# Transposes ahead of the maxima, output rows' transposes in the maxima's banks, and half a step between offset and scaling

## The chip, the cores and the metric

The kernel runs on one core of one Trainium2 chip. The metric is the device time of one execution in microseconds (us). The kernel before took 1583.12 us, the median of three runs (1580.37 to 1586.11).

The engines are named as in the profile: PE multiplies matrices (PEld loads its weights), DVE is the vector engine, ACT the scalar engine, POOL the general one, and SP issues DMAs. PE writes its results into PSUM, which has eight banks of 128 x 512 float32. DVE and ACT read them from there.

## What is computed

The input is `x` of 8 batches x 1024 rows x 256 columns. Every batch is computed by itself:

```python
xn = _layernorm(x, axis=-1)
s = _L0_attn_ref(xn, L0_attn_W_attn, L0_attn_b_attn, L0_attn_W_proj, L0_attn_b_proj)
g = _silu(_L0_ffn_ref(xn, L0_ffn_w_gate, L0_ffn_w_up, L0_ffn_w_down))
x = x + s * g
```

`_L0_attn_ref` is causal attention with 16 heads of 16 columns, with a rotation of queries and keys that (as the reference reads its axes) depends on the head, and a softmax. `_L0_ffn_ref` is a gated feed-forward with 768 hidden columns and integer weights: `silu(gate) * up`, then the down projection.

## The kernel before

**Groups and steps.** The 16 heads of a batch are worked on in 4 groups of 4, so there are 32 groups in all, strung in one chain. `attention` (L660) works on one group in 12 steps `n`: 4 blocks of keys for the first half of the queries, 8 for the second. A step has two pairs of heads, and a pair has two quarter steps, so a group has 48 quarter steps. The queries' exact row maxima are needed before the exponentials, so while group `i` computes its weights (`pw`, L562, then the exponential `e` on ACT, L569), the same quarter steps compute the maxima of group `i + 1` (`pm`, L504). `quarter_steps` (L641) spreads the 38 units of maxima over the 48 quarter steps, at most one in each. A unit is one bank of scores: PE writes it, DVE reduces it (L513 for a block of keys that lies wholly before the queries, L515 with the mask for the others).

**What a quarter step issues, in this order:** the weights of a bank; pieces of other work (`slot(weights)`); the unit of maxima, if there is one; in a few quarter steps a small transposition (below); again pieces of other work (`slot(maxima)`). The order is written out by hand, and each engine executes its own instructions in that order. At the end of a pair one entry of `vector` is run (a piece of the next batch's layer norm). After every second step the products of exponentials and values of two steps follow (`av`, L598).

**The small transposes.** `shift_queries` (L537) turns the row maxima of half of a group's queries into rows: one transpose `pq` (L540), a copy to `rows` on ACT (L542), and two small DMAs from SP into the queries' array `q_st` (L544). It runs twice per group, in the second quarter step of steps 2 and 7. `finish` (L611) takes the sums `avs` of a half of a group: four transposes `py` (L616), then on DVE a reciprocal `rec` (L618) and a product `y` (L619). It is called through `endings`, in the last quarter step of steps 1 and 5.

**Banks.** Eight banks are divided in four pools: two for `pw`, three for the maxima (`max_tile`, L72), one for `av`, and two for everything else (`fill_tile`, L75). `pq` and `py` take banks of the maxima. A tile can be written only when the earlier tile in its bank has been read by its last reader. `fill_tile` first calls `flush()`, which issues the DVE work that was put off in the list `later` (for example the gate `th`, L352, that reads a bank `ph`). `maxima` calls `flush()` too, behind its own reductions.

**The other work** is one long list `chain` of pieces, taken in order when they are due by the planner's costs (`slot`, L823): projections of the next batch (`pqk` L234, `pv` L267), the feed-forward (`ph` L325, whose readers are ACT L337 and L341 and then DVE L352; `pd` L379, read by ACT L390 and DVE L391), and the output of the batch before in four pairs of row tiles. `transpose_y` (L408) opens a pair: a DMA of `res`, four transposes `pyt` (L417) into one bank of the pool of two, and a copy `yT` on ACT (L423). `project_out` (L425) multiplies it (`po`, L432). Pairs 1, 2 and 3 are each followed in the chain by pieces of the feed-forward: pair 1 by `pd`, pairs 2 and 3 by `ph`.

**The norm of the next batch.** `norm_steps` (L94) returns a list of entries, one for each half step: eight of statistics (DVE), `first`, three `step` (POOL from the second batch on), `offset` (POOL, L127 and L128), and eight of `scale`, which run on ACT from the second batch on (L137) and read what `offset` wrote.

Of the kernel before, what the change touches and what calls it, by code (L numbers as in the profile page):

```python
# [35 lines left out]
def gated_block_kernel(ctx: ExitStack, tc: tile.TileContext, x, wqk, wv, bv, wp, bp, wg, wu, wd, rope, out):  # L36
# [3 lines left out]
    CC = C // P  # L40
# [23 lines left out]
    def flush(keep=0):  # L64
        while len(later) > keep:
            later.pop(0)()

    def cast(keep=0):
        while len(casts) > keep:
            casts.pop(0)()  # L70

    def max_tile(name):  # L72
        return ps_pm.tile([P, HALF], F32, tag="pm", name=name)

    def fill_tile(name):  # L75
        flush()
        return ps_fill.tile([P, HALF], F32, tag="fill", name=name)
# [16 lines left out]
    def norm_steps(b):  # L94


        stats = {}

        def one(t):
            if t == 0:  # L100
                stats["mv"] = small.tile([P, NT, 2], F32, tag="mv", name=f"mv_{b}")
            st = small.tile([P, 6], F32, tag="st", name=f"st_{b}_{t}")
            nc.vector.bn_stats(out=st, in_=xs[:, t, :])
            nc.vector.bn_aggr(out=stats["mv"][:, t, :], in_=st)

        def first():

            var, rstd, t = (small.tile([P, NT], F32, tag=tag, name=f"{tag}_{b}") for tag in ("var", "rstd", "newton"))
            stats["root"] = var, rstd, t
            nc.vector.tensor_scalar(var, stats["mv"][:, :, 1], LN_EPS, None, ALU.add)  # L110
            nc.vector.tensor_scalar(rstd.bitcast(I32), var.bitcast(I32), -0.5, float(0x5F3759DF), ALU.mult, ALU.add)

        def step():
            var, rstd, t = stats["root"]
            if b == 0:
                nc.vector.tensor_tensor(t, rstd, rstd, ALU.mult)
                nc.vector.scalar_tensor_tensor(t, t, -0.5, var, ALU.mult, ALU.mult)
                nc.vector.scalar_tensor_tensor(rstd, t, 1.5, rstd, ALU.add, ALU.mult)
                return
            nc.gpsimd.tensor_tensor(t, rstd, rstd, ALU.mult)  # L120
            nc.gpsimd.tensor_tensor(t, t, var, ALU.mult)
            nc.gpsimd.tensor_scalar(t, t, -0.5, 1.5, ALU.mult, ALU.add)
            nc.gpsimd.tensor_tensor(rstd, rstd, t, ALU.mult)

        def offset():
            _, rstd, t = stats["root"]
            nc.gpsimd.tensor_tensor(t, stats["mv"][:, :, 0], rstd, ALU.mult)  # L127
            nc.gpsimd.tensor_scalar(t, t, -1.0, None, ALU.mult)  # L128

        def scale(i):  # L130
            _, rstd, t = stats["root"]
            if b == 0:
                nc.vector.tensor_scalar(
                    xs[:, i, :], xs[:, i, :], stats["mv"][:, i, 0:1], rstd[:, i : i + 1], ALU.subtract, ALU.mult
                )
            else:
                nc.scalar.activation(  # L137
                    xs[:, i, :], xs[:, i, :], AF.Identity, bias=t[:, i : i + 1], scale=rstd[:, i : i + 1]
                )
            scaled[b] = i + 1  # L140

        tiles = range(NT)
        return [
            *[lambda t=t: one(t) for t in tiles],
            *[first, step, step, step],
            *([offset] if b else []),
            *[lambda t=t: scale(t) for t in tiles],
        ]

# [59 lines left out]
    class Batch:  # L209
# [198 lines left out]
        def transpose_y(self, pair):  # L408
            b = self.b
            assert self.complete[pair // 2] == GROUPS  # L410
            self.res[pair] = p2.tile([P, 2, C], F32, tag="res", name=f"res_{b}_{pair}")
            nc.sync.dma_start(out=self.res[pair], in_=x[b, ts(pair, 2 * P), :].rearrange("(t p) d -> p t d", p=P))
            py = fill_tile("pyt").rearrange("p (c n) -> p c n", c=CC)
            for c in range(CC):
                for i in range(2):
                    t = 2 * pair + i
                    nc.tensor.transpose(py[:, c, ts(i, P)], self.y[t // QT][:, t % QT, ts(c, P)], ident)  # L417
            if (b, pair) == (NB - 1, NT // 2 - 1):

                self.yT[pair] = pe.tile([P, 2, HALF], F32, tag="e", name=f"yT_{b}_{pair}")[:, :, : 2 * P]  # L420
            else:
                self.yT[pair] = p1.tile([P, CC, 2 * P], F32, tag="yT", name=f"yT_{b}_{pair}")
            nc.scalar.copy(self.yT[pair], py)  # L423
# [207 lines left out]
    def add_values(count):  # L631
        for _ in range(count):
            of, half, kb, es = waiting.pop(0)
            ending = of.values(half, kb, es)
            if ending:
                endings.append(ending)
# [23 lines left out]
    def attention(groups, at, plan, slot, vector):  # L660

        group = groups[at]
        after = groups[at + 1] if at + 1 < len(groups) else None
        loaded = groups[at + 2] if at + 2 < len(groups) else None
        plan = iter(plan)
        for n, (half, kb) in enumerate(group.weight_steps()):
            es = []
            for pair in range(2):
                e, banks = group.weights(half, kb, pair)
                es.append(e)  # L670
                for second, bank in enumerate(banks):
                    weights, maxima, units = next(plan)
                    if bank:
                        bank()
                    cast()
                    slot(weights)
                    for unit in units:
                        after.maxima(*unit)
                    if not units:
                        flush()  # L680
                    if pair == 0 and second and n == 2:
                        group.shift_queries(1)
                    if pair == 0 and second and n == QT + 3 and after:
                        after.shift_queries(0)
                    if pair == 1 and second and endings:
                        endings.pop(0)()
                    slot(maxima)
                if vector:
                    vector.pop(0)()
            waiting.append((group, half, kb, es))  # L690
            if len(waiting) == 3:
                add_values(2)
            for entry in delayed:
                entry[0] -= 1
            while delayed and delayed[0][0] <= 0:
                delayed.pop(0)[1]()
            if n == QT - 1 and after:
                after.shift_parts(0)
            if n == STEPS - 1 and after:
                after.shift_parts(1)  # L700
            if loaded:
                if n == QT - 1:
                    loaded.load(0, 0)
                elif n == 2 * QT - 1:
                    loaded.load(1, 0)
                elif n == STEPS - 1:
                    loaded.load(0, 1)
                    loaded.load(1, 1)
# [14 lines left out]
    def forward(exact, general=None):  # L723
# [88 lines left out]
        for b in range(NB):  # L812

            here = range(b * GROUPS, (b + 1) * GROUPS)
            for i in here:
                open_group(groups, batches, i + 2)
            plans = [quarter_steps(groups[i], groups[i + 1] if i + 1 < len(groups) else None) for i in here]
            total = sum(w + m for plan in plans for w, m, _ in plan) + sum(us for us, _ in chain[done[0] : marks[b + 1]])
            slots = 2 * sum(len(plan) for plan in plans)
            due, spent, at = [0.0], [0.0], [0]  # L820
            vectors = []

            def slot(before):  # L823
                due[0] += total / slots
                spent[0] += before
                at[0] += 1
                while (
                    done[0] < (marks[b + 1] if b + 1 < NB or batches[b].complete[0] == GROUPS else marks[b + 1] - 6)
                    and spent[0] + chain[done[0]][0] / 2 <= due[0]
                ):  # L830
                    spent[0] += chain[done[0]][0]
                    run(1)
                if at[0] == 8 and b < NB - 1:
                    if b:
                        load_x(b + 1)
                    vectors.extend([lambda: None] * 5 + norm_steps(b + 1))

            for i, plan in zip(here, plans):
                attention(groups, i, plan, slot, vectors)
                groups[i] = None  # L840
            run(marks[b + 1] - done[0])
# [160 lines left out]
```

## Time and profile before

| | |
|---|---|
| median of the runs | 1583.12 us |
| the profiled execution, its time / its span | 1587.18 / 1585.4 us |
| PE busy | 1507.6 us, 95% of the span |
| DVE busy | 1085.5 us, 68% |
| ACT busy | 959.4 us, 61% |
| POOL busy | 740.7 us, 47% |
| granted PE clock, mean | 0.990 |
| DMA, share of 16 engines | 43.4% for the main queue |
| `pq` L540: instructions, mean | 64, 271 ns |
| `py` L616: instructions, mean | 256, 274 ns |
| `pyt` L417: instructions, mean | 128, 272 ns |
| copies to `rows` L542 / `yT` L423, median | 250 / 587 ns |
| `rec` L618 / `y` L619, median | 250 / 424 ns |
| `scale` on ACT, L137: instructions, median | 56, 602 ns |

Busy is the union of an engine's instructions. A row of a group of instructions gives their number, the busy time, the mean of one in ns, and then the idle time of the engine just before them with what ended it. A line of the timeline gives start, duration, engine, line and operation, the tile written and those read, and in brackets the idle time before it with its releaser. Where one matmul follows another closely, their recorded spans overlap, so the distance between their starts says more than the durations.

### The profile page before, as it was taken

The page shows a single profiled execution, that of the slowest core. Times are in us where ns is not written, and L with a number is a line of the kernel's source. Part 1 is how long each engine was busy: PE and PEld are TensorE (multiplying, and loading weights), DVE is VectorE, ACT ScalarE, POOL GpSimd, SP SyncE. Part 2 cuts the span into 40 slices and gives each one's busy share as a digit, 9 for nine tenths or more (in the row PEclk, how much of TensorE's full clock was granted, in tenths as well). Part 3 has the DMA queues.
Part 4 walks back from the last instruction along what each step waited for, and adds up shares of the span by engine and source line. Part 5 has one row for each costly group of instructions (what it writes and reads, how often), then busy time and mean ns, then how long its engine had stood idle before and what let it go on. Part 6 is the DMA issues. An engine that isn't in the chain of part 4 may idle for free.

```text
span 1585.4 us, 29513 instructions
## 1 busy us (share of the span) xinstructions
PE 1507.6 (95%) x9801; PEld 1054.3 (66%) x9801; DVE 1085.5 (68%) x3284; ACT 959.4 (61%) x2076; POOL 740.7 (47%) x1443
## 2 busy tenths in 40 slices
PE   4889999999999999999999999999999999999997
PEld 2567667676677766776666766767666676666664
DVE  6876776767767677776667666776676767777742
ACT  2256665576656666566655766657665666656664
POOL 4554443554436443464434734355343544434353
PEclk9999999999999999999999999999999999999999
DMA  6812554334464255543346344444455335445301
GB/s 180 185 29 41 108 106 76 76 55 104 98 104 65 51 106 97 98 75 67 94 77 111 58 95 95 75 94 62 94 108 88 68 49 110 93 75 81 48 15 43
DMA packets 92086, 132.86 MB, mean 84 GB/s; under 512 B 13714, under 2 KB 41874, under 8 KB 91923
## 3 DMA queue, kind: packets, MB, share of 16 engines
q1 hardware_dynamic: 90944, 129.82, 43.4%
q8 instruction: 80, 1.31, 0.4%
q10 hardware_dynamic: 978, 1.05, 0.3%
q14 instruction: 84, 0.68, 0.2%
HBM read 87.82 MB, written 41.94 MB: 82 GB/s over the span
## 4 chain that ended last, share of the span: by engine, by line
PE 85%; DVE 4%; ACT 4%; POOL 2%; issue 2%; DMA 2%; SPq 1%; DVEq 0%; ACTq 0%; POOLq 0%
PE pw L562 20%; PE av L598 17%; PE pm L504 16%; PE ph L325 11%; PE pqk L234 6%; PE pd L379 6%; PE po L432 3%; PE pv L267 3%; ACT e L569 2%; PE py L616 2%; DVE trash L515 1%; DMA qk<-high 1%; PE pxt L225 1%; PE pq L540 1%; DVE low L249 1%
## 5 line engine op out<-in xcount | busy, mean ns | idle before, releaser
L569 ACT ACTIVATE e<-pw 128x512 f32<-128x512 f32 (+2 forms) x1280 | 678.7, 558 | 427.8 <-PE pw L562 396.8
L515 DVE CUSTOM_DVE_ANT_0 trash<-pm,mask_q 128x128 bf16<-128x128 f32 (+3 forms) x1024 | 501.3, 490 | 336.0 <-PE pm L504 297.0
L562 PE MATMUL pw<-q_st,k_st 67*128 67x512 f32 (+3 forms) x1536 | 554.3, 394 | 8.0 <-ACT e L569 5.5
L504 PE MATMUL pm<-k_st,q_st 65*128 65x512 f32 (+3 forms) x1536 | 520.9, 377 | 6.9 <-DMA qk<-high 3.7
L562 PEld LDWEIGHTS pw<-q_st,k_st 67*128 67x128 f32 x1536 | 277.7, 189 | 205.6 <-issue 100.3
L576 POOL TENSOR_SCALAR_AFFINE_SELECT e<-e 128x256 f32<-128x256 f32 x512 | 206.6, 408 | 437.0 <-ACT e L569 435.3
L513 DVE TENSOR_REDUCE top_far<-pm 128x1 f32<-128x512 f32 x512 | 338.6, 684 | 70.3 <-PE pm L504 69.1
L504 PEld LDWEIGHTS pm<-k_st,q_st 65*128 65x128 f32 x1536 | 279.6, 191 | 57.7 <-issue 17.2
L598 PE MATMUL av<-e,v_sb 128*32 128x512 f32 (+3 forms) x3072 | 293.1, 499 | 0.3 <-POOL e L576 0.3
L356 POOL TENSOR_TENSOR th<-th,ups 128x256 f32<-128x256 f32 x192 | 140.5, 732 | 231.5 <-DVE th L352 225.4
L598 PEld LDWEIGHTS av<-e,v_sb 128*32 128x32 f32 x3072 | 81.0, 110 | 133.6 <-issue 100.6
L360 POOL TENSOR_TENSOR h_low<-th,h_high 128x256 fp32r<-128x256 f32 x192 | 140.7, 733 | 15.4
L234 PE MATMUL pqk<-xnT,wqk_sb 128*128 128x512 f32 x256 | 133.9, 609 | 0.3 <-DVE bqk_sb L912 0.3
L325 PE MATMUL ph<-xnT_high,wg_sb 128*128 128x256 f32 x384 | 102.1, 288 | 12.0 <-DVE th L352 9.0
L379 PE MATMUL pd<-wd_sb,h_high 128*128 128x256 f32 x384 | 99.0, 286 | 7.9 <-ACT yT L423 4.7
L352 DVE SCALAR_TENSOR_TENSOR th<-th,ph 128x256 f32<-128x256 f32 x192 | 79.7, 415 | 31.2 <-ACT ups L341 30.8
L325 PE MATMUL ph<-xnT_high,wu_sb 128*128 128x256 f32 x384 | 101.1, 285 | 0.0
L379 PE MATMUL pd<-wd_sb,h_low 128*128 128x256 f32 x384 | 98.3, 285 | 1.7 <-POOL h_low L360 1.7
L325 PE MATMUL ph<-xnT_low,wg_sb 128*128 128x256 f32 x384 | 99.2, 281 | 0.0
L325 PE MATMUL ph<-xnT_low,wu_sb 128*128 128x256 f32 x384 | 99.1, 280 | 0.0
L337 ACT ACTIVATE th<-ph 128x256 f32<-128x256 f32 x192 | 73.7, 384 | 39.3 <-PE ph L325 34.5
L515 DVE DVE_READ_ACCUMULATOR2_ANT top<- 128x1 f32 x1024 | 85.0, 83 | 0.2 <-issue 0.2
(98 smaller groups left out, 1669.6 us busy)
## 6 DMA issues: line engine op xcount, KB each, us to landing
q_st<-qk SPq DMA_DIRECT2D x256, 128.0 KB, 4.1
k_st<-qk SPq DMA_DIRECT2D x256, 128.0 KB, 5.4
qk<-high SPq DMA_DIRECT2D x64, 256.0 KB, 2.9
qk<-low SPq DMA_DIRECT2D x64, 256.0 KB, 2.8
xs<-in_x SPq DMA_DIRECT2D x16, 512.0 KB, 8.3
res<-in_x SPq DMA_DIRECT2D x32, 256.0 KB, 4.9
out<-res SPq DMA_DIRECT2D x32, 256.0 KB, 2.3
q_st<-rows SPq DMA_DIRECT2D x128, 8.0 KB, 2.1
```

The lines of the kernel that those rows point to most:

```text
L234: nc.tensor.matmul(pt, wqk_sb[:, c, ts(i, P)], xnT[:, c, ts(half, HALF)], start=(c == 0), stop=(c == CC - 1),)
L325: nc.tensor.matmul(pt, self.weights[up][:, c, ts(hc, P)], part[:, c, ts(quarter, QU)], start=(c == 0 and i == 0), stop=(c == CC - 1 and i ...
L356: nc.gpsimd.tensor_tensor(h, th, ups, ALU.mult)
L360: nc.gpsimd.tensor_tensor(low, th, high.bitcast(F32), ALU.subtract)
L379: nc.tensor.matmul(pt, h[:, ts(i, P)], self.weights[2][:, hc, :], start=(hc == 0 and n == 0), stop=(hc == HC - 1 and n == len(hs) - 1),)
L504: nc.tensor.matmul(pm[:, ts(i, n)], self.q_st[half][:SHIFT, head, at], self.k_st[keys][:SHIFT, head, :n], start=True, stop=True,)
L513: nc.vector.tensor_reduce(self.top_far[:, head, qt - QT : qt - QT + 1], pm, AX.X, ALU.max)
L515: nc.vector.tensor_tensor_reduce(trash[:, :n], pm[:, ts(i, n)], mask_q[:, HALF - n :], 1.0, MASKED, ALU.add, ALU.max, self.top[:, head, qt ...
L562: nc.tensor.matmul(pw[:, ts(i, n)], self.k_st[kb // QT][:, head, ts(kb % QT, P)], self.q_st[half][:, head, lo:], start=True, stop=True,)
L569: nc.scalar.activation(e[:, first : first + count, lo:], pw[:, : count * n].rearrange("p (a n) -> p a n", n=n), AF.Exp,)
L576: nc.gpsimd.affine_select(out=e[:, :, lo : lo + P], in_=e[:, :, lo : lo + P], pattern=[[0, 2], [1, P]], compare_op=ALU.is_ge, fill=0.0, ba ...
L598: nc.tensor.matmul(self.av[ts(j, SLOT), lo:], vs[self.batch.b % 2][:, kb, at : at + SLOT], es[j // 2][:, j % 2, lo:], start=(kb == 0), sto ...
```

## The change

Three edits. In `norm_steps` an empty entry is put between `offset` and the first `scale`, so that every `scale` comes one half step later. In `transpose_y` the four transposes take a bank of the maxima's three in place of one of the pool of two, and, since `max_tile` doesn't flush, what lies in `later` isn't issued there. In `attention` the maxima of a quarter step are issued behind `shift_queries` and `endings` in place of ahead of them; where a quarter step has no unit, the `flush()` moves with them.

```diff
@@ norm_steps
             *[first, step, step, step],
-            *([offset] if b else []),
+            *([offset, lambda: None] if b else []),
             *[lambda t=t: scale(t) for t in tiles],
@@ transpose_y
-            py = fill_tile("pyt").rearrange("p (c n) -> p c n", c=CC)
+            py = max_tile("pyt").rearrange("p (c n) -> p c n", c=CC)
@@ attention
                     cast()
                     slot(weights)
-                    for unit in units:
-                        after.maxima(*unit)
-                    if not units:
-                        flush()
                     if pair == 0 and second and n == 2:
                         group.shift_queries(1)
                     if pair == 0 and second and n == QT + 3 and after:
                         after.shift_queries(0)
                     if pair == 1 and second and endings:
                         endings.pop(0)()
+                    for unit in units:
+                        after.maxima(*unit)
+                    if not units:
+                        flush()
                     slot(maxima)
```

## The prediction

> **What bounds the kernel now.** I read the page's first two parts, then the windows of whole batches, the groups of PE with their idle time, and the timeline around each idle place. PE is the bound. In a batch of the middle it is busy for 184.4 of 189 us, and no other engine reaches 71% (columns: window, length, then busy time of PE, PEld, DVE, ACT, POOL):
>
> ```profile
> PE 1507.6 (95%) x9801; PEld 1054.3 (66%) x9801; DVE 1085.5 (68%) x3284; ACT 959.4 (61%) x2076; POOL 740.7 (47%) x1443
> ```
>
> ```profile
> 371.00:560.00 189.00, 184.41 (x1224) 130.99 (x1224) 132.83 (x407) 119.60 (x260) 90.36 (x178) 1.00 0.46 84
> ```
>
> So 4.6 us of a batch are idle on PE. Its groups say where (last column: idle before, then releasers):
>
> ```profile
> L504 PE MATMUL pm<-k_st,q_st 65*128 65x512 f32 x768 | 333.5, 441 | 2.9 <-DVE top_far L513 1.4 <-DVE top L515 0.5 <-ACT rows L542 0.3
> L325 PE MATMUL ph<-xnT_high,wg_sb 128*128 128x256 f32 x384 | 102.1, 288 | 12.0 <-DVE th L352 9.0 <-ACT yT L423 3.0
> L379 PE MATMUL pd<-wd_sb,h_high 128*128 128x256 f32 x384 | 99.0, 286 | 7.9 <-ACT yT L423 4.7 <-POOL h_high L359 3.2
> L616 PE MATMUL py<-ident,avs 128*128 128x128 f32 x256 | 39.0, 274 | 2.8 <-DVE top L515 2.0 <-ACT avs L608 0.7
> L540 PE MATMUL pq<-ident,parts 128*32 128x128 f32 x64 | 17.4, 271 | 9.3 <-DVE y L619 8.9
> ```
>
> The change touches all of these. The same places recur every 189 us. The worst `pq`, PE then DVE; it waits for `y` of two quarter steps ago, and the rest of PE's queue waits behind it:
>
> ```profile
> 416.28 0.46 PE L504 MATMUL pm<-k_st,q_st 65*128 65x512 f32 x1
> 417.61 0.27 PE L540 MATMUL pq<-ident,parts 128*32 128x128 f32 x1 [0.88 <-DVE y L619]
> ```
>
> ```profile
> 416.10 0.75 DVE L249 SCALAR_TENSOR_TENSOR low<-pqk,bqk_sb,high 128x512 fp32r<-128x512 f32 x1
> 416.76 0.25 DVE L618 RECIPROCAL rec<-py 128x16 f32<-128x16 f32 x1
> 417.04 0.42 DVE L619 TENSOR_TENSOR y<-py,rec 128x256 f32<-128x256 f32 x1
> 417.38 0.55 DVE L515 CUSTOM_DVE_ANT_0 trash<-pm,mask_q 128x384 bf16<-128x384 f32 x1
> ```
>
> The three waits behind output transposes, of pairs 1, 2 and 3, and on ACT the cause of the last:
>
> ```profile
> 465.88 0.39 PE L379 MATMUL pd<-wd_sb,h_high 128*128 128x256 f32 x1 [0.78 <-ACT yT L423]
> ```
>
> ```profile
> 482.14 0.39 PE L325 MATMUL ph<-xnT_high,wg_sb 128*128 128x256 f32 x1 [0.49 <-ACT yT L423]
> ```
>
> ```profile
> 497.01 0.60 PE L417 MATMUL pyt<-ident,y 128*128 128x128 f32 x4
> 497.37 0.48 PE L504 MATMUL pm<-k_st,q_st 65*128 65x512 f32 x1
> 499.16 0.39 PE L325 MATMUL ph<-xnT_high,wg_sb 128*128 128x256 f32 x1 [1.31 <-DVE th L352]
> ```
>
> ```profile
> 496.95 0.60 ACT L137 ACTIVATE xs<-xs,newton,rstd 128x256 f32<-128x256 f32 x1 [0.94 <-POOL newton L128]
> ```
>
> These idles, 0.53 + 0.88 + 0.03 (three of a batch's four `pq` of step 2), 0.30 (`py`), 0.78, 0.49 and 1.31, are 4.32 of the 4.6 us.
>
> **What the Trainium skill says.** "Perfetto Trace Analysis", section Identifying the Most-Contended Engine, calls matmul busy time no good measure, since matmuls are pipelined. The trace agrees: a 65x512 `pm` lasts 441 ns on the mean, but where nothing waits the next matmul starts 0.23 us later (the `pm` at 296.35, its `pq` at 296.58). So I price a stall by start to start, not by the idle column. "PSUM — Partial Sum Buffer", section Engine vs sequencer instructions: DVE and ACT are strict queues and matmuls start in program order. The trace agrees: nothing overtakes `pq` in 1.33 us. The same page, section PSUM bank collisions, wants waits by bank; `pq` starts 0.15 after `y` ends at 417.46.
>
> **The change part by part.** No instruction is added or removed; only order, banks and waits change. A release costs about 0.13 us.
>
> *The order in a quarter step.* At steps 1 and 2 the maxima's banks go, before, u7, `py`, u8, u9, `pq`, u11 (u7: the unit of quarter step 7); after, `py`, u7, u8, `pq`, u9, u11. With three banks `pq` takes that of `py` either way, but on DVE `rec` and `y` (0.25 + 0.42) now stand ahead of u7's reduction (0.56) and of what `flush` issues (`low`, 0.75). u9 then takes u7's bank, so the wait passes to u9. I replay the four groups of a batch with the trace's durations and compare the start of the `pw` behind the pair:
> - 417: DVE frees u6 at 415.4, so `y` ends near 416.17, u7 near 416.65. `pq` goes at 416.3 without a wait, u9 at 416.80, `pw` at 417.03 against 417.64: +0.61.
> - 371: `y` 370.07, u7 370.56, u9 370.70, `pw` 370.95 against 371.22: +0.27.
> - 464: u7 now waits for what `py` waited for (u5, 461.96), u8 for u6, u9 (464.05) for u7; `pw` 464.29 against 464.18: -0.11.
> - 513: no wait before; u9 waits for u7 (513.53): -0.18.
>
> Together 0.59 of the 2.45 us that start to start shows here (`pq` 0.70, 1.10, 0.20, 0; `py` 0.45). At steps 5 and 7 there is no wait now (`pq` 0.23 after the unit) and I see none coming: DVE stood idle for 1.10 us before the unit beside `pq` at 296.58. SP's two DMAs for `q_st` (2.1 us to landing) go up to 0.3 us earlier and ahead of the flush's own DMAs; their reader comes two steps later.
>
> *The bank of `pyt`.* Pair 1: the next `pd` started 0.05 after `yT` ended (465.83), so it had got the transpose's own bank. After, it takes a free one of the two and goes at 464.94, 0.11 behind the last transpose: +0.94. Pair 2: `ph` loses its wait, but `pyt` follows three units closely and its maxima's bank is the one whose reduction ends near 481.55; it waits 0.84, and `ph` starts near 482.25 against 482.14: -0.11. Pair 3: `ph` waited for the gate L352 of the tile before it, since `pyt` held the other bank. After, that bank was free since 496.16: `ph` at 497.61, +1.55. The omitted flush puts L352 behind one reduction (0.68), at about 498.5, as late as now (498.68), and nobody waits. Pair 0: a bank is free (reduction over at 449.55), 0.
>
> *The empty entry.* ACT no longer stands 0.94 us for `offset`; the queue behind it (an exponential, L337, L341, the copy `yT`) comes that much earlier. PE's price of it is the same 1.55 above, so I count nothing more in those batches, and 0.3 in the first, where no output follows. The last `scale` stays over 10 us ahead of its reader (`pxt` at 529.67).
>
> *Sum.* 0.59 + 0.94 - 0.11 + 1.55 = 2.97 us a batch. Six batches have the pairs behind them in this form: 17.8. The first gives 0.59 + 0.3. In the last the transposes lie elsewhere and didn't stall; two of them now meet reductions (I read 0.3 and 0.4 at 1418 and 1434), against some 0.4 won at `pq`: -0.3. In all 18.4 us. I keep back a tenth for time that PE then waits for ACT at `pw`: 17 us. The profiled execution's 1587.18 (1.8 around its span) becomes 1570; the same off the median gives 1566.
>
> The bounds: only the ACT-freed and DVE-freed waits that I named return, 2 us a batch lost again: 6 us in all; every stall goes, 5.6 us in seven batches: 39, of which I believe at most 30.
>
> **The rivals.**
> - *Gains half eaten* (wait moved, not removed): pair 3's unit at 497.37 or u9 gets the bank that ACT frees, or PE meets ACT at `pw`. For it: three of four replays end at another wait. Then 4 to 10 us: 1573 to 1579, say 1576.
> - *All stalls go*, since the units meet freer banks than I replayed: 22 to 34 us: 1549 to 1561.
> - *Slower.* `pq` and `pyt` are read by ACT. If the unit issued right behind `pq` is given `pq`'s own bank, it waits for the copy to `rows`, which ends 0.56 to 0.70 us after `pq` starts, some 0.55 of it uncovered; now units follow `pq` by 1 to 1.5 us and the wait is hidden (only 0.3 us behind L542 above). In all 62 places that is 34 us lost against 18 won: 1599. It decides from 18/0.55, 33 places, that is, from the whole of step 7. Against it: there DVE idles and an older bank is free.
> - *No effect*, within 0.3% (4.7 us, about what a measurement can tell): gains of part two only, given back by u9.
>
> **How the numbers follow.** Forecast 0.58 (1560 to 1572), half eaten 0.20, all gone 0.07, no effect 0.06, slower 0.09. Faster is 0.58 + 0.20 + 0.07 = 0.85. The range 1557 to 1579 takes in the forecast, nearly all of the half-eaten case and a part of the next, and leaves the slower one out.
>
> **What would show it.** `pq` starts 0.03 to 0.1 after its forerunner; idle behind `y` L619 leaves PE's groups and some turns up at `pm`, behind DVE. The `yT` and `th` releasers leave `ph` and `pd`; pair 2's `pyt` shows a wait for `top_far`. ACT's idle behind POOL L128 is gone. A `pm` behind ACT L542 or L423 with more than 5 us proves me wrong.

## The result, and the profile after

The kernel after takes 1565.04 us, the median of six runs (1561.48 to 1568.21). The kernel before, with three more runs than ahead of the prediction, took 1583.76 (six runs, 1580.37 to 1592.91). The ratio is 0.987, with a 95% interval of 0.9846 to 0.9894: 18.7 us, where 17 were forecast. The profiled execution took 1564.28 us and its span is 1562.5.

Part 1 of the page after, in the same columns as before, and then the window of one middle batch, which lasts 185.80 us in place of 189.00:

```profile
PE 1506.6 (96%) x9801; PEld 1057.9 (68%) x9801; DVE 1083.7 (69%) x3284; ACT 958.6 (61%) x2076; POOL 740.4 (47%) x1443
```

```profile
368.00:553.80 185.80, 184.53 (x1227) 131.48 (x1225) 132.72 (x407) 119.51 (x261) 90.34 (x178) 1.00 0.47 87
```

PE does as much as before. Only its idle time went, from 4.6 us of this batch to 1.3. The groups of PE after say which:

```profile
L504 PE MATMUL pm<-k_st,q_st 65*128 65x512 f32 x768 | 340.7, 451 | 5.4 <-DVE top_far L513 2.2 <-DVE top L515 0.8 <-ACT rows L542 0.7
L325 PE MATMUL ph<-xnT_high,wg_sb 128*128 128x256 f32 x384 | 100.4, 283 | 0.8 <-DVE th L352 0.8
L379 PE MATMUL pd<-wd_sb,h_high 128*128 128x256 f32 x384 | 98.0, 284 | 3.3 <-POOL h_high L359 3.3
L417 PE MATMUL pyt<-ident,y 128*128 128x128 f32 x128 | 20.0, 278 | 4.5 <-DVE top_far L513 3.9 <-DVE y L619 0.6
L540 PE MATMUL pq<-ident,parts 128*32 128x128 f32 x64 | 17.6, 274 | 0.0
```

`pq` lost all of its 9.3 us, `ph` 11.2 of 12.0, and `pd` the 4.7 behind `yT`. Two waits grew: `pyt` now stands 3.9 us behind a reduction of maxima, and `pm` 5.4 in place of 2.9. So some of the waiting passed on, as the prediction's replays had it. These are places that it named, now in the timeline of PE after (first a `pq` of the second batch and its unit; then the worst `pq` of a middle batch with its unit; then the openings of pairs 1, 2 and 3, each `pyt` with the matmul that had waited behind it):

```profile
182.81 0.27 PE L540 MATMUL pq<-ident,parts 128*32 128x128 f32 x1
183.42 0.50 PE L504 MATMUL pm<-k_st,q_st 65*128 65x512 f32 x1 [0.34 <-ACT rows L542]
...
413.96 0.27 PE L540 MATMUL pq<-ident,parts 128*32 128x128 f32 x1
414.30 0.50 PE L504 MATMUL pm<-k_st,q_st 65*128 65x512 f32 x1
...
461.45 0.66 PE L417 MATMUL pyt<-ident,y 128*128 128x128 f32 x4
461.87 0.36 PE L379 MATMUL pd<-wd_sb,h_high 128*128 128x256 f32 x1
...
477.53 0.66 PE L417 MATMUL pyt<-ident,y 128*128 128x128 f32 x4 [0.62 <-DVE top_far L513]
...
478.25 0.28 PE L325 MATMUL ph<-xnT_high,wg_sb 128*128 128x256 f32 x1
...
493.02 0.60 PE L417 MATMUL pyt<-ident,y 128*128 128x128 f32 x4
...
493.69 0.28 PE L325 MATMUL ph<-xnT_high,wg_sb 128*128 128x256 f32 x1
```

No bracket stands at `pq`, `pd` or either `ph`. Of the places named in the middle batch one is left with a bracket, pair 2's `pyt` (0.23 us of `pw` behind ACT stand in both kernels and were not named). The wait that the prediction passed on to u9 shows in the distance alone: 0.34 us from `pq` to its unit at 414.30, where 0.11 is the distance without a wait (460.68 to 460.79). The releaser of `pyt` is on DVE, whose timeline after shows the reduction that ends near 477.5 (two of them in one line), and, for the first place, `y` already behind it when the unit's reduction starts:

```profile
413.35 0.42 DVE L619 TENSOR_TENSOR y<-py,rec 128x256 f32<-128x256 f32 x1
413.69 0.55 DVE L515 CUSTOM_DVE_ANT_0 trash<-pm,mask_q 128x384 bf16<-128x384 f32 x1
...
476.81 1.26 DVE L513 TENSOR_REDUCE top_far<-pm 128x1 f32<-128x512 f32 x2
```

To see what each place is worth I laid the two traces side by side by their 1536 `pw` matmuls (L562), which come in the same order in both, and read where the distance between the two changes. In a middle batch it changes, from before to after, by +0.25 (group starting at 371), +0.67 (417), -0.20 (464) and -0.20 us (513) at the `pq` of step 2, by +0.08 at the second `pw` behind each of these four, by +0.93 at pair 1, by -0.75 and then +0.75 at pair 2, and by +1.59 at pair 3. There is one more loss, -0.20 behind the `py` of step 5 in the first of these groups (at 386 us before, 384 after). The rest are steps of at most 0.13, most of which cancel. Together it is 3.3 us.

A batch is 192 of these `pw`. I count them from the start of the third group on (its second `pw`), so that every length runs from the middle of one batch to the middle of the next; what is called the second batch here begins there. These lengths leave the start of the kernel out, its first two groups and what comes ahead of them. The start takes 172 to 181 us in the profiles, in no order of the edits, and goes with the clock of PE in it: it takes over 178 us in the four profiles where the clock is at half for 27 us or more of it, and under 177 in the nine with 24 us or less.

The table has the lengths for all kernels of this study. The ratios aren't quotients of its medians, since each is to runs of the kernel before on the same chip. Their median was 1583.76 us beside the kernel after, 1589.35 beside the first four experiments (order, bank, empty entry, order and bank), 1587.63 beside the three with only the endings ahead, only the shifts ahead, or pair 2 later, and 1586.48 beside the other three.

| kernel | third to seventh batch, us | median of its runs, us | ratio to before, 95% interval |
|---|---|---|---|
| before | 189.1 to 190.9 | 1583.76 | |
| before, second profile | 189.1 to 191.4 | 1583.94 (one run) | |
| order alone | 188.2 to 188.6 | 1579.23 | 0.9952 (0.9933 to 0.9971) |
| bank alone | 186.8 to 187.1 | 1568.85 | 0.9887 (0.9856 to 0.9917) |
| empty entry alone | 188.0 to 188.2 | 1574.5 | 0.993 (0.9904 to 0.9955) |
| order and bank | 185.8 to 186.1 | 1568.19 | 0.9886 (0.9854 to 0.9918) |
| bank and empty entry | 186.8 to 187.2 | 1568.46 | 0.9888 (0.9862 to 0.9915) |
| all three (after) | 185.8 to 186.0 | 1565.04 | 0.987 (0.9846 to 0.9894) |
| after, second measurement | 185.8 to 186.1 | 1563.31 | 0.9851 (0.9823 to 0.9878) |
| after, only the endings ahead | 185.5 to 185.7 | 1562.01 | 0.984 (0.9791 to 0.9889) |
| after, only the shifts ahead | 186.2 to 186.8 | 1569.14 | 0.9878 (0.9835 to 0.992) |
| after, pair 2 one piece later | 185.1 to 185.3 | 1561.01 | 0.9837 (0.9794 to 0.988) |
| after, endings only and pair 2 later | 184.8 to 185.1 | 1559.51 | 0.9837 (0.9809 to 0.9865) |

### The profile page after: what moved, and what is told of

It reads as the page before. It is cut to its first block, busy times and chain, and to the rows that moved or that the text cites. A ratio compares the mean times of both kernels' runs of the same rounds, so it can differ in the third digit from the quotient of the medians.

```text
span 1562.5 us, 29525 instructions
## 1 busy us (share of the span) xinstructions
PE 1506.6 (96%) x9801; PEld 1057.9 (68%) x9801; DVE 1083.7 (69%) x3284; ACT 958.6 (61%) x2076; POOL 740.4 (47%) x1443
## 4 chain that ended last, share of the span: by engine, by line
PE 85%; DVE 7%; ACT 2%; POOL 2%; DMA 1%; issue 1%; SPq 0%; ACTq 0%; DVEq 0%; POOLq 0%
PE pw L562 20%; PE av L598 17%; PE pm L504 17%; PE ph L325 10%; PE pqk L234 7%; PE pd L379 6%; PE pv L267 3%; PE po L432 3%; DVE top_far L513 2%; DVE trash L515 2%; ACT e L569 2%; PE py L616 1%; DVE st L103 1%; PE pyt L417 1%; DMA qk<-high 1%
## 5 line engine op out<-in xcount | busy, mean ns | idle before, releaser
L562 PE MATMUL pw<-q_st,k_st 67*128 67x512 f32 (+3 forms) x1536 | 546.5, 389 | 7.6 <-ACT e L569 5.2
L504 PE MATMUL pm<-k_st,q_st 65*128 65x512 f32 (+3 forms) x1536 | 527.5, 382 | 9.6 <-DMA qk<-high 3.3
L562 PEld LDWEIGHTS pw<-q_st,k_st 67*128 67x128 f32 x1536 | 281.1, 189 | 202.5 <-issue 91.9
L598 PE MATMUL av<-e,v_sb 128*32 128x512 f32 (+3 forms) x3072 | 289.5, 494 | 0.3 <-POOL e L576 0.3
L337 ACT ACTIVATE th<-ph 128x256 f32<-128x256 f32 x192 | 73.8, 385 | 42.6 <-PE ph L325 37.0
```

The costliest lines, as they stand in the source:

```text
L504: nc.tensor.matmul(pm[:, ts(i, n)], self.q_st[half][:SHIFT, head, at], self.k_st[keys][:SHIFT, head, :n], start=True, stop=True,)
L562: nc.tensor.matmul(pw[:, ts(i, n)], self.k_st[kb // QT][:, head, ts(kb % QT, P)], self.q_st[half][:, head, lo:], start=True, stop=True,)
L598: nc.tensor.matmul(self.av[ts(j, SLOT), lo:], vs[self.batch.b % 2][:, kb, at : at + SLOT], es[j // 2][:, j % 2, lo:], start=(kb == 0), sto ...
```

## The experiments

**Each edit by itself.** The first kernel is the kernel before with the order of the quarter step alone:

```diff
                     slot(weights)
-                    for unit in units:
-                        after.maxima(*unit)
-                    if not units:
-                        flush()
                     if pair == 0 and second and n == 2:
...
                         endings.pop(0)()
+                    for unit in units:
+                        after.maxima(*unit)
+                    if not units:
+                        flush()
                     slot(maxima)
```

> The kernel before with the order in a quarter step alone (small transposes ahead of the maxima). My theory, the waits are handed on to the unit behind pq: a batch of the middle, 189.1 us before, becomes 0.6 to 0.9 us shorter, in all 4 to 6 us, ratio 0.996 to 0.998; the idle behind y L619 at pq is gone, the waits behind pyt stand as before (pd 0.9, ph 0.7 and 1.5 us, start to start). Rival, the order is what does most of the change: 10 us or more, ratio under 0.994. A second question: where pair 3 still stalls 1.5 us, PE's granted clock should fall to half for some us behind it in some batches, as it did in two batches of the kernel before; if it never does, that loss has another cause.

It took 1579.23 us. The third batch went from 189.1 to 188.2: 0.9 us, as the theory had it; the ratio, 0.9952, lies just below the 0.996 that it gave. In its groups of PE, `pq` waits no more, and `ph` waits as it did in the kernel before (12.0 there):

```profile
L325 PE MATMUL ph<-xnT_high,wg_sb 128*128 128x256 f32 x384 | 101.6, 286 | 11.7 <-DVE th L352 8.7 <-ACT yT L423 3.0
L540 PE MATMUL pq<-ident,parts 128*32 128x128 f32 x64 | 17.5, 274 | 0.0
```

The steps at the four groups are those of the kernel after to 0.01 us (+0.24, +0.67, -0.19, -0.20). So the order's share is its own, and owes nothing to the other edits.

The second has the bank of the output transposes alone:

```diff
-            py = fill_tile("pyt").rearrange("p (c n) -> p c n", c=CC)
+            py = max_tile("pyt").rearrange("p (c n) -> p c n", c=CC)
```

> The kernel before with the output rows' transposes in the maxima's banks alone. My theory, pair 3's ph waits because pyt holds the other bank of two, so the bank alone takes the whole wait, though ACT still stands 0.94 us for offset: pair 1 wins 0.9, pair 2 nothing, pair 3 1.5 us, 2.4 us in six batches, 14 to 16 us in all with the clock, ratio 0.990 to 0.9915. Rival, ACT's standing still is the cause at pair 3 and the bank only helps pair 1: 5 to 6 us, ratio 0.9965.

1568.85 us, and a third batch of 186.9: 2.2 us. The steps are +0.73 at pair 1, -0.83 and +0.76 at pair 2, and +1.59 at pair 3. In its groups the stall at `pq` is as it was, and `pyt` has got the new one:

```profile
L417 PE MATMUL pyt<-ident,y 128*128 128x128 f32 x128 | 20.0, 278 | 5.1 <-DVE top_far L513 3.9 <-DVE y L619 0.6
L540 PE MATMUL pq<-ident,parts 128*32 128x128 f32 x64 | 17.5, 274 | 9.1 <-DVE y L619 8.7
```

The third has the empty entry alone:

```diff
-            *([offset] if b else []),
+            *([offset, lambda: None] if b else []),
```

> The kernel before with the empty entry between offset and scale alone. My theory, ACT's 0.94 us is the head of the queue that ends at pair 3's ph: the wait there falls from 1.5 to 0.3 to 0.6 us, 1.0 to 1.2 us in six batches, 6 to 8 us in all, ratio 0.995 to 0.996; so this edit and the bank win the same time at pair 3. Rival, L352 comes no earlier, since DVE or POOL holds it too: under 2 us, ratio 0.999 or more.

1574.5 us, and a third batch of 188.0. In a middle batch there is one step only, +1.11 at pair 3, and in the groups of PE the wait for the gate fell from 9.0 to 1.9:

```profile
L325 PE MATMUL ph<-xnT_high,wg_sb 128*128 128x256 f32 x384 | 102.1, 288 | 4.9 <-ACT yT L423 3.0 <-DVE th L352 1.9
```

So the place of `scale` made 1.11 us at `ph`, but not all of it is ACT's wait for `offset`, which lasted 0.94. In the kernel before, `L337`, which the gate needs, ran at 497.93, behind that wait, the `scale` at 496.95 and an exponential. Here the first `scale` comes behind it, at 492.69, and `L337` waits for PE alone (the timeline of ACT, then the `ph` of PE):

```profile
492.15 0.38 ACT L337 ACTIVATE th<-ph 128x256 f32<-128x256 f32 x1 [0.30 <-PE ph L325]
...
493.40 0.39 PE L325 MATMUL ph<-xnT_high,wg_sb 128*128 128x256 f32 x1 [0.20 <-DVE th L352]
```

The edit took both away, the wait and the `scale` itself; this run doesn't part them.

**Do the edits add up?** The batches' gains of the three alone are 0.9 + 2.2 + 1.1 = 4.2 us. Together they give 3.3. The fourth kernel has order and bank, without the entry.

> The order and the bank together, without the empty entry. My theory, the empty entry adds at most 0.3 us in a few batches once the bank is moved: within 2 us of the kernel with all three, ratio 0.987 to 0.989. Rival, the three edits add up: 6 us slower than all three, ratio 0.991. In the trace: ACT idle of about 0.9 us in seven batches behind POOL L128, and no wait of ph behind it.

Its batches last 185.8 us, those of the kernel after. As expected, ACT still stands for 5.8 us behind L128 in its seven batches, and it costs a middle batch nothing. A later kernel has bank and entry, without the order.

> The kernel after without the order's edit: the bank of the output transposes and the empty entry, units ahead of the small transposes as before. Theory: the empty entry adds nothing beside the bank, since both take away the same stall of pair 3; middle batch 186.8 to 187.0, as with the bank alone (186.8), and the order is worth 1.0 us a batch in the kernel after. Rival: the empty entry and the order are what overlaps; then the batch is 186.0 to 186.3.

Its batches last 186.8, those of the bank alone. Both say the same: beside the bank the entry is worth nothing in a middle batch. Entry and bank take away the same stall, one by making the gate earlier, the other by no longer needing the gate's bank. Order and bank (0.9 + 2.2 = 3.1, measured 3.3) touch different places and add up; the 0.2 over lies at pair 1, as the account of the bank below says.

**Which half of the order pays?** Two kernels undo one half of the order's edit in the kernel after. In the first only the endings stay ahead of the maxima, and the two `shift_queries` go behind the unit again:

```diff
-                    if pair == 0 and second and n == 2:
-                        group.shift_queries(1)
-                    if pair == 0 and second and n == QT + 3 and after:
-                        after.shift_queries(0)
                     if pair == 1 and second and endings:
                         endings.pop(0)()
                     for unit in units:
                         after.maxima(*unit)
                     if not units:
                         flush()
+                    if pair == 0 and second and n == 2:
+                        group.shift_queries(1)
+                    if pair == 0 and second and n == QT + 3 and after:
+                        after.shift_queries(0)
```

> The kernel with all three edits, but shift_queries behind the maxima again, so that only finish stays ahead of them. My theory of the order: what wins is that rec and y stand ahead of a reduction and of the flush on DVE, which is finish's part alone. pq then takes the bank of the unit ahead of it and a batch of the middle is 185.8 us as with both, or up to 0.4 us less. Rival, pq's own place is what wins: the waits behind y return and the batch takes 186.5 us or more.

Its batches last 185.5 us: 0.3 less than with both halves. The timeline of its PE at the worst `pq`, to be laid beside the lines of the kernel after at 413.96 above:

```profile
413.96 0.44 PE L504 MATMUL pm<-k_st,q_st 65*128 65x512 f32 x1
414.40 0.27 PE L540 MATMUL pq<-ident,parts 128*32 128x128 f32 x1
414.43 0.48 PE L562 MATMUL pw<-q_st,k_st 67*128 67x256 f32 x2
```

Once the endings go first, `y` is over in time and a bank is free at 413.96. Either `pq` or the unit can have it; the other waits for the next reduction, to about 414.3. If `pq` takes it, 0.34 us pass until the unit starts and another 0.34 until `pw`, which in the kernel after starts at 414.64. If the unit takes it, its own columns fill the wait, `pq` is followed by `pw` within 0.03, and `pw` starts at 414.43.

The other kernel keeps the shifts ahead and puts the endings behind the unit:

```diff
-                    if pair == 1 and second and endings:
-                        endings.pop(0)()
                     for unit in units:
                         after.maxima(*unit)
                     if not units:
                         flush()
+                    if pair == 1 and second and endings:
+                        endings.pop(0)()
```

> The kernel with all three edits, but finish behind the maxima again, so that only shift_queries stays ahead of them. My theory: y ends as late as in the kernel before, pq only meets the wait 0.23 us earlier, and the batch is 186.6 to 186.9 us, what the bank alone gives, idle on PE behind y L619 at pq again. Rival, pq's own place is what wins: 186.0 us or less.

Its batches last 186.2 us, and one of them 186.8: between what the two theories gave, and the idle time isn't where I had put it. `pq` shows no idle. Its unit waits, a little for `y` (1.7 us in all) and more for the copy of `pq` itself on ACT. First the line of its groups of PE, then of its timeline at the same place:

```profile
L504 PE MATMUL pm<-k_st,q_st 65*128 65x512 f32 x768 | 339.0, 449 | 8.8 <-ACT rows L542 4.8 <-DVE y L619 1.7 <-DVE top_far L513 1.4
```

```profile
418.11 0.27 PE L540 MATMUL pq<-ident,parts 128*32 128x128 f32 x1
...
418.72 0.50 PE L504 MATMUL pm<-k_st,q_st 65*128 65x512 f32 x1 [0.34 <-ACT rows L542]
```

The copy to `rows` ran from 418.42 to 418.68, and the unit starts 0.04 later: it got `pq`'s own bank, while that of `py` was still read by `y`, to 419.24. That is the mechanism of the prediction's slower rival, at 13 of 62 places (a fourteenth wait of this kind, near 60 us, is in every kernel), with 0.61 us from `pq` to the unit where 0.11 is the distance without a wait. So the order owes its gain to the endings, and moving the shifts is worth something only when the endings stay where they were.

**The wait that took the place of pair 2's.** The kernel after, with one more piece of the feed-forward ahead of pair 2's transposes:

```diff
-                chain += o0 + d0[:2] + t1 + d0[2:] + o1 + u1[:4] + t2 + u1[4:6] + o2 + u1[6:10] + t3 + u1[10:]
+                chain += o0 + d0[:2] + t1 + d0[2:] + o1 + u1[:5] + t2 + u1[5:6] + o2 + u1[6:10] + t3 + u1[10:]
```

> The kernel with all three edits, and pair 2's transposes moved one piece of the feed-forward later in the chain (behind the first half of a hidden tile in place of ahead of it). My theory, the 0.6 to 0.75 us that pyt of pair 2 now waits is only DVE's lag behind three closely spaced units: one piece later the reduction of the oldest is over, and a batch of the middle falls from 185.8 to 185.1 to 185.3 us, 3 to 4 us in all, ratio against the kernel before 0.985. Rival, the wait turns up again behind the moved transposes (po for the copy yT, or the next unit for its bank): 185.7 us or more.

Its batches last 185.1 us, 0.7 less. The comparison of `pw` shows one step in a middle batch, +0.73 at pair 2, and in its groups of PE the wait of `pyt` for the maxima is gone:

```profile
L417 PE MATMUL pyt<-ident,y 128*128 128x128 f32 x128 | 20.0, 278 | 0.7 <-DVE y L619 0.6 <-DVE top_far L513 0.2
```

That is what "Perfetto Trace Analysis" of the Trainium skill, section Optimization Strategy, says of a bubble that repeats: it can mean that there isn't PSUM enough for the next tile. Here a bank more wasn't needed, only a request for it at another place.

**Both together.** The last two edits in one kernel, with the kernel after beside it on the same chip:

> The kernel after with both edits of the runs before it that gained: only the endings ahead of the maxima (shift_queries behind the unit again), and the opening of pair 2 one piece later. Theory: the two gains lie at different places (the group starts at 371, 417 and 513, 0.3 us a batch; pair 2's transposes, 0.7 us a batch) and add up: a middle batch of 184.8 us (185.8 in the kernel after, less 0.3, less 0.7), about 6 us below the kernel after on the same chip. Rival: the freed time is met by the next wait, and the batch stays at 185.1 or above, as with the pair's edit alone. PE's busy time of such a batch is 184.5, so less than 184.5 is not to be had.

> The kernel after, unchanged, as the measure for the two kernels beside it on the same chip: middle batches of 185.8 us again if the batch is set by the program's order, and a start of the kernel (up to the first weights of the second batch) between 172 and 181 us, as the profiles so far spread.

The kernel after has batches of 185.8 us again, and a start of 175 us. In the kernel with both edits a middle batch lasts 184.8 us, so the gains add up. The window of one of them:

```profile
355.20:540.00 184.80, 184.23 (x1226) 131.18 (x1226) 132.63 (x407) 119.77 (x262) 90.08 (x179) 1.00 0.47 87
```

0.6 us of idle are left on PE in the records. Its waits can cost more than that: at the worst `pq` before, 0.88 us of idle were 1.10 from start to start. Nor is the 184.5 us of busy time a floor, as I had expected, since here it is 184.23. The medians are 1559.51 us (1555.31 to 1564.81) against 1563.31 (1561.78 to 1566.96) of the kernel after. The difference of 3.8 us is below the 6 that six batches would give, and the two intervals overlap; the batches separate the kernels, the medians hardly do.

## Why the prediction was right

The bound, the places, the signs of the larger steps and the sum were right. By the prediction's own steps, for a middle batch:

| step | predicted, us | measured, us |
|---|---|---|
| order, group at 417 | +0.61 | +0.67 |
| order, group at 371 | +0.27 | +0.25 |
| order, group at 464 | -0.11 | -0.20 |
| order, group at 513 | -0.18 | -0.20 |
| order, second `pw` behind each | not seen | +0.32 |
| order, behind `py` of step 5 in one group | 0 | -0.20 |
| bank, pair 1 | +0.94 | +0.93 |
| bank, pair 2 | -0.11 | 0.00 |
| bank, pair 3 | +1.55 | +1.59 |
| empty entry, beside the bank | 0 | 0 |
| smaller steps, 0.13 at most | not seen | +0.16 |
| sum | 2.97 | 3.32 |

- *The order.* The replays held to 0.1 us in all four groups, losses too. What they left out is small and regular: before, `pq` stood right ahead of `pw`, and the second `pw` came 0.20 us behind the first; after, the unit stands there, and it comes 0.12 behind. Four times 0.08 is the 0.32 in the table. I had priced a transpose by its own distance and not by what it does to the matmul after next. At step 5 I saw no wait coming, and in one group there is one: the second unit behind `py` still has a free bank, and the third has to take that of `py`: it starts at 383.14, 0.15 us after `y` ends. One price of the replays was too even: a release at 0.13 us each, where the traces show 0.15 behind `y` and 0.05 or 0.04 behind the copies on ACT.
- *The bank.* Pair 2 went as foreseen: the wait moved from `ph` to `pyt` (0.62 us idle there now), and nothing was won. Pair 1 gives 0.93 with the order and 0.73 without it: without it the second `pw` ahead goes 0.20 earlier in that group, and `pyt` stands for the same 0.2 (0.39 behind that `pw` in place of 0.20). So this loss is paid once, at u9 or at `pyt`, and belongs to the bank as much as to the order.
- *The empty entry.* "PE's price of it is the same 1.55 above, so I count nothing more in those batches": shown for a middle batch from both sides, by order with bank (185.8 with the entry and without) and by the bank (186.8 both ways). Alone it is worth 1.1 us a batch, more than the 0.94 us wait that the prediction named; the `scale` itself moved too. ACT's idle ahead of `scale`, 6.3 us before, is 0.0 after.
- *First and last batch.* I gave the first 0.89 and the last -0.3. The last, from the middle of the seventh batch to the last `pw`, won 0.5: two of its `pyt` lost 0.36 and 0.29, as foreseen, but step 2 of its groups won more. The first can't be told: the start of the kernel spreads by some 9 us among the profiles. The second batch won 2.4 and not 2.97: there the unit behind a `pq` did get `pq`'s own bank (183.42 above), which cost 0.66.
- *The tenth kept back* for waits of `pw` on ACT wasn't needed. Forecast from the unreduced 18.4 us, the time would have been 1564.7.
- *The profiled execution* was to become 1570 and became 1564.28. The prediction's sum, 18.4, stands against 22.9 us there. From the batches, 2.4 in the second, five times 3.3, and 0.5 in the last are 19.4. Of the other 3.5 us 3.1 were not the change's own waits, but a lower clock in two batches of the kernel before, to which the last section comes. The prediction had no term for it. That the medians differ by 18.7 us, near to the 17, is in part luck: the tenth was kept back for a wait that didn't come, and the medians lie below what the batches of the profiles give.

Of the rivals, *gains half eaten* was right that waits move and wrong about the size: they did, at u9 and at pair 2's `pyt`, and the replays had them in already. *Slower* needed the unit behind `pq` to get `pq`'s bank. In the kernel after that happens twice, at 62 us, as in every kernel, and at 183 us, 0.34 us of idle each. That it can happen more often is shown by the kernel with only the shifts ahead. Its price, 0.61 less 0.11, is 0.50 us a place, close to the 0.55 of the prediction.

Not settled: why the allocation gives the unit `pq`'s bank at some places and another bank at others. The traces show when a tile starts and who released it, and not which bank it has.

## What to carry to other kernels

Price a wait in a rotation of banks by replaying who takes which bank next, and count the wait's new place before counting its removal: of the edits here, pair 2's won nothing, and the shifts' took back 0.3 us a batch of what the endings' gave. Where one of two instructions has to wait for a bank, let the one with more work of its own go first (here 0.2 us at each of four places a batch). Two edits that take away the same stall from its two sides must be measured together: alone they promise it twice (4.2 us a batch here, of which 3.3 came).

## What the runs showed of the hardware

The kernel before has two batches of 190.9 and 190.8 us, the sixth and the seventh, among others of 189.1 to 189.6. In both the stall at pair 3, of 1.33 us, is followed by a stretch at half of PE's clock. The trace's records of the clock change only in steps of 3.41 us, so I cut the windows of the kernel before at those steps, to 0.05 us: the one with the stall of the sixth batch, the one behind it, then those with the stall of the fifth and of the fourth batch, where the clock stayed (the last three columns are granted clock, DMA share and GB/s):

```profile
1064.48:1067.89 3.41, 2.08 (x15) 1.59 (x13) 1.92 (x4) 3.00 (x8) 3.17 (x8) 1.00 0.07 24
1067.89:1071.30 3.41, 3.41 (x18) 0.72 (x17) 0.70 (x2) 0.59 (x2) 1.91 (x4) 0.51 0.00 0
876.76:880.17 3.41, 2.24 (x21) 1.07 (x21) 1.72 (x4) 2.19 (x5) 3.18 (x7) 1.00 0.01 2
685.59:689.00 3.41, 2.09 (x16) 1.70 (x14) 2.03 (x4) 2.90 (x7) 3.17 (x8) 1.00 0.10 35
```

With the clock at half, sixteen `av` matmuls take 3.21 us in place of 1.71. The second profile of the kernel before was to tell chance from place:

> The kernel before, unchanged, for a second profile. Theory: the half clock behind pair 3's stall comes by chance of where the stall falls, so it shows in other batches than the sixth and seventh or in none, and a batch without it lasts 189.1 to 189.6 us. Rival: it belongs to those two batches, and they last 190.8 us again with half clock at 1068 and 1259 us.

It has the half clock once, in the fifth batch, behind a stall of 1.65 us of which the most falls in one window (PE busy for 1.76 of 3.41 us), and that batch lasts 191.4 us. The sixth and the seventh last 189.3 and 189.2. So it belongs to no batch. In the two profiles 3 of 12 such stalls were followed by it, at 1.6 to 1.8 us each against the same batch without it, and in the kernel with the order alone, where the stall is still there, none of six: 3 of 18, one in a profile on the mean. After the change PE has no such stall, and no middle batch shows a lowered clock.

The Trainium skill, "TensorE: Matmul & The Clock Gate", sections Part 1 (the HAM clock gate) and HAM oscillation, tells of a full and a half clock and of a free-running window of some 3.4 us. The steps agree. Its rule, that idle gaps above some 3.4 us are what lowers the clock, does not: half clock followed two gaps of 1.3 us and one of 1.65. The share of PE's busy time isn't the whole rule either. Over all thirteen profiles, between the first and the last weights, 21 windows at full clock have PE busy for less than 0.6, and 20 of them were followed by half clock. The other holds the most of the fifth batch's stall, of 1.61 us, in the kernel with the order alone, and the clock stayed (that window and the next):

```profile
873.63:877.04 3.41, 2.01 (x17) 1.08 (x21) 1.72 (x4) 2.42 (x6) 3.18 (x7) 1.00 0.01 2
877.04:880.45 3.41, 3.41 (x25) 2.56 (x18) 1.41 (x4) 1.99 (x6) 1.01 (x3) 1.00 0.00 0
```

Of the windows with PE busy for 0.61 some were, as above (2.08 us was, 2.09 wasn't). And in the last batch three of the profiles have a half clock behind a window in which PE is recorded as busy for 0.95. What the hardware counts is left open. The three stalls that half clock followed cost about twice their length, which no count of idle time shows.
